# Moving the depthwise blocks behind the half-height products in a two-layer convolution kernel

## The chip, the cores and the metric

The kernel runs on one core of one Trainium2 chip, in float32 throughout. The metric is the device time of one launch in microseconds. A core has five engines that run their own instruction streams in order and wait for each other through semaphores: TensorE (PE in the profile, its weight loads PEld), VectorE (DVE), ScalarE (ACT), GpSimd (POOL) and SyncE (SP). DMAs are issued from the queues of SP, ACT and POOL.

## The reference

The input x has 8 images of 96 by 96 pixels and 192 channels. Two residual layers follow one another:

```python
x = x + L0(_gn(x), ...)   # _gn: group norm over 32 groups
x = x + L1(_gn(x), ...)
# L0: proj = x @ W_in + b_in (192 -> 384 channels); local = 3x3 depthwise conv
#     mixed = 0.25*(four exponential scans of local: left, right, down, up) + local
#     layer norm over channels; @ W_out + b_out (384 -> 192)
# L1: y = 7x7 depthwise conv + dw_bias; layer norm over the 192 channels
#     y = gelu(y @ w0 + b0) (192 -> 768); (y @ w1 + b1) * gamma (768 -> 192)
```

## The kernel before

The program is one launch, written out by hand: every queue receives its instructions in the order in which the Python code issues them (`tc.manual_schedule()`). Its stages follow one another on TensorE.

**First pass, scans and second pass.** The first pass projects to 384 channels, the next stage does the 3x3 convolution and the scans. The second pass (line 1219 on, "stage C") takes 192 steps, 3.94 us each. A step transposes three tiles to form squares, multiplies by W_out (`project_c`, L1141), and one step later `scale_c` makes the inverse deviation (VectorE, then a power on GpSimd, L1170) and `finish_c` (L1175, VectorE) scales the sums, adds the residual and frees the sums' PSUM banks; there are banks for two steps. Between `scale_c` and `finish_c` the list `steps` hands out side work, one entry a step: `bn_stats` of three groups (two in the last entry), and, once, the five single steps of `norm_c(0, ...)` (line 980: means, squares, powers, shift, spread), which make the second layer's group norm for the first half of the images.

**Depthwise blocks (stage D).** The 7x7 convolution is done in 32 blocks of 12 channels (`todo`: two halves of the images, 16 blocks each). A block n has its rows loaded (`load_raw`, three tiles t) and its band of weights (`load_band`), its rows scaled by the group norm (`scale_steps`: 24 scalings in three tiles of eight, and one copy of the band, L964), six convolutions (`conv_d`, each 24 matmuls of 64x64 tiles, L1337, and two evacuations on ScalarE, L1347), and its result stored (`store_d`). The scalings are on VectorE (L960) for most blocks and on ScalarE (L958) for block 1 and for blocks 19 and up (N1 = 19). Nineteen blocks run before the products begin, one a pass of the loop at line 1622.

**Products (stage E).** The rest of layer 1 runs in 72 units u, two to a tile n of y (loop at line 1700). For a unit, `norm_steps_e` gives seven steps of the layer norm: sums, mean, center (VectorE), square (ScalarE, L1501), squares (VectorE), powers (a VectorE sum, then a power on GpSimd, L1513, 5.4 us), scale (VectorE). They run two units ahead. `turn_in` then transposes y into yT (L1534). `first_layer` multiplies by w0 in parts: for each part first the full-height products (L1549: 128 rows by 512 columns), then the half-height products (L1559: the remaining 64 channels, two matmuls at once on the two halves of the array), then the gelus on ScalarE (L1568). `second_layer(u - 1, k)` for k = 0 to 3 multiplies by w1 (L1579); VectorE adds the residual r (L1590) and POOL issues the store. In the first 36 units `first_layer` has three parts and uses a pool of six PSUM banks, since the convolutions hold the other two; in the other 36 it has two parts and all eight banks.

**Inlaid blocks.** The last 13 depthwise blocks (19 to 31) are worked off inside stage E through the list `slots`: nine entries a block, three of scalings (called R below) and six of one convolution each (called C), and one store at the end. `slot()` is called five times a unit from u = 1 on, and each call takes the next entry, whatever it is: after the first part of `first_layer`, and after each of the four `second_layer` calls. So convolutions stand at all five places in turn.

**The passage from D to E.** In block 17's pass (n == NI + 1) the scalings of block 18 come first, then sums, mean and center of unit 0. Then the six convolutions, then the loads of tile 1 of y (`y_1`: 41 steps, eight of which at the end, the left-over channels, go through POOL). In block 18's pass unit 0's square, squares and powers, unit 1's sums, mean and center, and unit 0's scale are issued behind the third convolution. Then the rows of block 19 are loaded (POOL), and the residual r of tile 0 behind them (`load_r(0, nc.gpsimd)`); `bias_r(0)` adds a bias to it on POOL (L1430) before unit 0's loop.

Of the kernel before, what the change touches and what calls it, by code (L numbers as in the profile page):

```python
# [101 lines left out]
def conv_blocks_kernel(  # L102
# [31 lines left out]
    nc = tc.nc  # L134
# [9 lines left out]
    GS = D // GROUPS  # L144
# [437 lines left out]
    NI = len(place)  # L582
# [308 lines left out]
    NT = 3  # L891
# [53 lines left out]
    def scale_steps(n):  # L945

        hf, i = todo[n]
        steps = []

        def scale(t, k, b):  # L950
            if n not in xins:
                make_xin(n)
            c = slice(k * GS, (k + 1) * GS)
            sc, sh = (s1[:, hf, b, e, 2 * i + k : 2 * i + k + 1] for e in range(2))
            to = xins[n][:, t, b, c].rearrange("q c (a v) -> q a c v", a=NV)
            of = raws[n, t][:, b, :, c]
            if n == 1 or n >= N1:
                nc.scalar.activation(to, of, AF.Identity, bias=sh, scale=sc)  # L958
            else:
                nc.vector.tensor_scalar(to, of, sc, sh, ALU.mult, ALU.add)  # L960

        def spread():
            g, band = i % 2, bands[n]
            nc.vector.tensor_copy(  # L964
                band[(1 - g) * 64 : (2 - g) * 64], band[g * 64 : (g + 1) * 64]
            )

        for t in range(NT):
# [76 lines left out]
    with ExitStack() as ph:  # L1045
# [173 lines left out]
        with tc.manual_schedule():  # L1219
# [15 lines left out]
            for u in range(n_u + 1):  # L1235
# [23 lines left out]
                if u < n_u:  # L1259
# [7 lines left out]
                    for j in range(NJ3):  # L1267
# [1 line left out]
                        turn_c(mt, pt, j, range(0 if u else NC - 1, NC))  # L1269
                        project_c(mt, pos[j], j, ms[j])  # L1270
                        square_c(pt, pos[j], var, j)
                if steps:
                    for step in steps.pop(0):
                        step()
                if held is not None:
                    n, v = divmod(u - 1, WQ)
                    if v == 0:
                        x1c = xps[1 - n % 2].tile([128, NJ3, D, WQ], F32, tag="x1c", name="x1c")
                    finish_c(x1c, v, held[0], rs, held[2])
                    if v == WQ - 1:  # L1280
                        steps += group_steps(x1c, n)
                        stores += [
                            lambda x=x1c, n=n, j=j, q=q: store_c(x, n, j, q)
                            for j in range(NJ3)
                            for q in range(NX)
                        ]
                held = (pos, var, xr) if u < n_u else None
            for step in first_d:
                step()
# [313 lines left out]
    with tc.manual_schedule():  # L1603
        with tc.tile_pool(name="d_own", bufs=1, side="right", **by_tile) as own:
# [12 lines left out]
                NI - 5: y_0[:1],  # L1617
                NI: [y_0[1 + b * 8 + q] for q in (5, 7) for b in range(NH)]
                + y_0[1 + NH * 8 :],
                NI + 1: y_1,  # L1620
            }
            for n in range(N1):
                if n + 2 < N1:
                    for t in range(NT):
                        load_raw(n + 2, t)
                    if n:
                        load_band(n + 2)
                if n:
                    store_d(n - 1)
                if n >= 3 and norms:  # L1630
                    norms.pop(0)()
                if n == 10:
                    make_weights(bank())
                steps = scale_steps(n + 1) if n + 1 < N1 else []
                between, last = [], []
                if n == NI + 1:
                    chain = norm_steps_e(0)
                    steps += chain[:3]
                    chain = chain[3:]
                elif n == NI + 2:  # L1640
                    nxt = norm_steps_e(1)
                    between = chain[:3] + nxt[:3] + chain[3:]
                    last = nxt[3:4]
                    chain = nxt[4:]
                for step in steps:
                    step()
                for c in range(GS):
                    conv_d(n, c)
                    for step in main_y.get(n, [])[2 * c : 2 * c + 2]:
                        step(nc.gpsimd)  # L1650
                    if c == 2:
                        for step in between:
# [12 lines left out]
        tp = ctx.enter_context(tc.tile_pool(name="e_t", bufs=2, side="right", **by_tile))  # L1665

# [1 line left out]
        for n in range(N1, len(todo)):  # L1668
            more = n + 1 < len(todo)
            scales = scale_steps(n)  # L1670
            per_t = len(scales) // NT
            slots += [after + scales[:per_t], scales[per_t : 2 * per_t], scales[2 * per_t :]]
            if more:
                for t in range(NT):
                    slots[t - 3].append(lambda n=n, t=t: load_raw(n + 1, t, nc.scalar if n > N1 else None))
            slots += [[lambda n=n, c=c: conv_d(n, c, ps_y)] for c in range(GS)]
            if more:
                slots[-1].append(lambda n=n: load_band(n + 1, nc.scalar))
            after = [lambda n=n: store_d(n)]
        slots.append(after)  # L1680
# [12 lines left out]
        load_r(0, nc.gpsimd)  # L1693
        for k in range(3):
            turn_in(0, k)
        for step in chain[:2]:
# [2 lines left out]
        bias_r(0)  # L1699
        for u in range(n_u + 1):  # L1700
            n, t = divmod(u, per)
            early_half = u < n_u // 2
            parts, pool = (3, ps_h) if early_half else (2, None)
            if not early_half:
# [20 lines left out]
            if not early_half:  # L1725
# [63 lines left out]
```

## Time and profile before

The three runs of the kernel took 5416.11, 5424.39 and 5430.3 us; the median is 5424.39 us.

| | |
|---|---|
| profiled execution, own time | 5428.47 us |
| its span, first to last instruction | 5426.5 us |
| granted TensorE clock, mean | 0.986 |
| TensorE busy in the span | 97% |
| VectorE, ScalarE, GpSimd busy | 64%, 48%, 44% |
| second pass (C), first to last projection | 1801.9 to 2591.8 us |
| depthwise blocks before the products (D) | 2592.1 to about 2902 us |
| products (E), first L1549 to last L1579 | 2922.4 to 5420.4 us |
| last inlaid convolution matmul starts at | 3880.5 us |

A group of instructions in the profile is named by its line and by what it writes and reads ("L1579 PE MATMUL hp<-w1g,g"); a wait is "who waited <- whom it waited for". A matmul in float32 appears as two instructions, so a count of matmuls in the profile is twice that in the code. Ends of matmuls are modelled, so this text counts TensorE's time from start to start.

### The profile page before, as it was taken

What the parts mean: (1) busy time and instruction counts of PE and PEld (TensorE: products, weight loads), DVE (VectorE), ACT (ScalarE), POOL (GpSimd) and SP (SyncE); (2) the same over time, 40 slices, a digit from 0 to 9 for tenths busy, and PEclk for the clock granted to TensorE, in tenths of its full rate; (3) what the DMA queues carried; (4) which work ended last, traced back from release to release, by engine and by line L of the source; (5) the groups of instructions that cost most, each with busy time, mean ns of one, the idle gap of its engine ahead of it and who ended that gap; (6) DMA issues with size and microseconds to landing.
All of it is one profiled execution on the core that took longest, in us unless ns stands there. A gap on an engine that the chain in (4) does not pass through costs nothing. (4 is left out here: it accounts for less than half of the span.)

```text
span 5426.5 us, 107918 instructions
## 1 busy us (share of the span) xinstructions
PE 5247.6 (97%) x42206; PEld 3346.3 (62%) x42206; DVE 3455.9 (64%) x6722; ACT 2581.9 (48%) x5765; POOL 2405.4 (44%) x2129
## 2 busy tenths in 40 slices
PE   6999999999999999999787999999999999999999
PEld 4666643333333799999454666666666666666667
DVE  6555539999999555555556555555566666566654
ACT  2444447777777566565434444454433333323232
POOL 1111128888888555555335222233233333333332
PEclk9999989999999999999898999999999999999999
DMA  7999869999999799899998455545433233332331
GB/s 221 285 286 277 251 183 239 247 240 244 246 243 246 230 306 308 273 301 312 282 308 206 119 137 135 131 120 138 108 79 78 80 81 85 87 92 80 81 78 41
DMA packets 784651, 1015.33 MB, mean 187 GB/s; under 512 B 322359, under 2 KB 658432, under 8 KB 782096
## 3 DMA queue, kind: packets, MB, share of 16 engines
q1 hardware_dynamic: 671432, 633.30, 44.3%
q0 software_dynamic: 86896, 336.90, 18.9%
q10 hardware_dynamic: 25816, 38.25, 3.1%
q8 instruction: 334, 5.47, 0.4%
q14 instruction: 173, 1.42, 0.1%
HBM read 603.70 MB, written 420.03 MB: 189 GB/s over the span
## 5 line engine op out<-in xcount | busy, mean ns | idle before, releaser
L1579 PEld LDWEIGHTS hp<-w1g,g 128*128 128x128 f32 x6912 | 1117.9, 190 | 140.7 <-issue 78.3
L1579 PE MATMUL hp<-w1g,g 128*128 128x192 f32 x6912 | 1174.9, 329 | 0.0
L1568 ACT ACTIVATE g<-hp,b0g 128x512 f32<-128x512 f32 x864 | 519.8, 693 | 1214.8 <-PE hp L1559 1191.9
L1598 POOL DMA_DIRECT2D out_dram<-xo x288 | 211.6, 735 | 1536.8 <-DVE xo L1590 1496.9
L1590 DVE TENSOR_TENSOR xo<-hp,r 128x384 f32<-128x384 f32 x288 | 229.0, 795 | 1002.2 <-PE hp L1579 998.7
L1549 PE MATMUL hp<-yT,w0w 128*128 128x512 f32 x1728 | 779.2, 597 | 22.1 <-DVE yT L1534 21.9
L1141 PE MATMUL po<-wc,mt 128*128 128x193 f32 x3456 | 667.4, 329 | 7.4 <-DVE x1c L1175 7.3
L688 PE MATMUL pl<-pin,band 34*32 34x380 f32 (+1 forms) x13824 | 636.6, 494 | 9.6 <-DMA pin<-PL_d 4.0
L775 POOL TENSOR_TENSOR mo<-mo,z 128x768 f32<-128x768 f32 x285 | 594.6, 2086 | 4.8 <-ACT mo L713 0.6
L1141 PEld LDWEIGHTS po<-wc,mt 128*128 128x128 f32 x3456 | 556.8, 192 | 9.0 <-DVE x1c L1175 8.6
L1549 PEld LDWEIGHTS hp<-yT,w0w 128*128 128x128 f32 x1728 | 321.2, 190 | 382.3 <-issue 350.5
L721 DVE TENSOR_TENSOR_SCAN z<-decay,loc 128x768 f32<-128x768 f32 x288 | 505.9, 1757 | 61.6 <-ACT loc L697 33.0
L730 DVE TENSOR_TENSOR_SCAN z<-decay,z 128x768 f32<-128x768 f32 x288 | 498.4, 1731 | 0.1
L1337 PE MATMUL hp<-xin,band 63*64 63x372 f32 (+1 forms) x4608 | 412.7, 496 | 70.9 <-ACT yo L1347 26.9
L688 PEld LDWEIGHTS pl<-pin,band 34*32 34x32 f32 x13824 | 234.4, 108 | 393.4 <-issue 386.7
L709 PE MATMUL pa<-loc,mix 128*32 128x384 f32 x3456 | 436.5, 498 | 0.0
L712 PE MATMUL pa<-last,down 96*32 96x384 f32 x1152 | 431.4, 498 | 1.0 <-ACT mo L713 1.0
L1559 PE MATMUL hp<-yT,w0w 64*128 64x512 f32 x1728 | 419.5, 611 | 0.0
L1513 POOL TENSOR_TENSOR rs<-tot,neg_half 32x32 f32<-32x32 f32 x72 | 395.6, 5494 | 46.1 <-DVE tot L1511 45.3
L1347 ACT ACTIVATE yo<-hp,dwb 128x384 f32<-128x384 f32 x384 | 197.1, 585 | 423.4 <-PE hp L1337 290.2
L697 ACT COPY loc<-pl 128x384 f32<-128x384 f32 x576 | 248.2, 483 | 312.3 <-PE pl L688 312.3
L395 PE MATMUL pm<-xT,win 128*128 128x384 f32 x1152 | 392.2, 491 | 0.0
(159 smaller groups left out, 7276.0 us busy)
## 6 DMA issues: line engine op xcount, KB each, us to landing
P<-po POOLq DMA_DIRECT2D x96, 1152.0 KB, 9.7
pin<-P SPq DMA_DIRECT2D x190, 576.0 KB
mt<-M SPq DMA_DIRECT2D x192, 384.0 KB
xq<-in_x_dram SPq DMA_DIRECT2D x96, 576.0 KB
xr<-in_x_dram SPq DMA_DIRECT2D x192, 288.0 KB
X<-x1c SPq DMA_DIRECT2D x144, 384.0 KB
out_dram<-xo POOLq DMA_DIRECT2D x288, 192.0 KB, 2.4
r<-X SPq DMA_DIRECT2D x35, 1536.0 KB
```

The lines of the kernel that those rows point to most:

```text
L688: nc.tensor.matmul(pls[g][at * RB : (at + 1) * RB, :, lo:hi], band[rows, c, kh, :], pin[rows, c, :, NJ - 1 - j, lo + kh - 1 : hi + kh - 1] ...
L709: nc.tensor.matmul(pa[at], mix[:, i, at], loc[:, q], start=True, stop=True)
L712: nc.tensor.matmul(pa[at], down[:, to], last[:, q], start=True, stop=True)
L721: nc.vector.tensor_tensor_scan(zf, decay_f, loc.rearrange("p q n -> p (q n)"), 0.0, ALU.mult, ALU.add)
L730: nc.vector.tensor_tensor_scan(zr, decay_f, zr, 0.0, ALU.mult, ALU.add)
L775: eng.tensor_tensor(m, m, z, ALU.add)
L1141: nc.tensor.matmul(po, mt[:, m, j * 128 : (j + 1) * 128], wc[:, m], start=(m == 0), stop=(m == NC - 1),)
L1337: nc.tensor.matmul(pys[g][k * 64 : (k + 1) * 64, :, lo:hi], band[rows, k * GS + c, d * ZS : d * ZS + 64], xin[rows, :, :, k * GS + c, lo + ...
L1549: nc.tensor.matmul(hps[m, q], w0w[:, 0, m * 128 : (m + 1) * 128], yT[:, 2 * q], start=True, stop=False,)
L1559: nc.tensor.matmul(hps[m, q], w0w[p, 1, m * 128 : (m + 1) * 128], yT[p, 1], start=False, stop=True,)
L1568: nc.scalar.activation(g[:, m, q], hps[m, q], AF.Gelu, bias=b0g[:, m : m + 1], scale=1.0)
L1579: nc.tensor.matmul(po[:, q], g[:, m, q, k * 128 : (k + 1) * 128], w1g[:, m], start=(m == 0), stop=(m == NE - 1),)
```

## The change

There are four edits.

1. **Kinds of slots and new places.** Entries of `slots` are marked "rows" or "conv", and a call of `slot` takes the next entry only if its kind is among those that it names. Convolutions may now stand behind each of the three parts of `first_layer`, that is, right behind half-height products, and behind `second_layer(u - 1, 2)`. Rows may stand behind `second_layer` 0, 1, 2 and 3. The loads that `slot` also issued are issued by `some()` at the five old places.
2. **When the three parts end.** `first_layer` has three parts, and six banks, as long as `slots` is not empty at the start of a unit, instead of up to unit 35.
3. **The passage from D to E.** The last eight scalings of block 18 go from VectorE to ScalarE and are issued two behind each of the first four convolutions of block 17. Unit 0's square, squares and powers, unit 1's sums, mean and center, and unit 0's scale are issued before the convolutions of block 18, not behind the third. The eight left-over loads of y's tile 1 on POOL go from the end of block 17's pass to the end of block 18's, behind the powers. The rows of block 19 are loaded behind r of tile 0, not ahead of it.
4. **Second pass.** An entry of `steps` that holds a single step (the five of `norm_c(0)`) is issued behind `finish_c`, the others ahead of it as before.

```diff
-            if n == 1 or n >= N1:
+            if n == 1 or n >= N1 or (n == N1 - 1 and t == NT - 1):
                 nc.scalar.activation(to, of, AF.Identity, bias=sh, scale=sc)
...
-                if steps:
-                    for step in steps.pop(0):
+                now = steps.pop(0) if steps else []
+                if len(now) > 1:
+                    for step in now:
                         step()
                 if held is not None:
...
+                if len(now) == 1:
+                    now[0]()
                 held = (pos, var, xr) if u < n_u else None
...
-                NI + 1: y_1,
+                NI + 1: y_1[:-8],
...
                 if n == NI + 1:
                     chain = norm_steps_e(0)
-                    steps += chain[:3]
+                    per_t = len(steps) // NT
+                    between = steps[-1 - per_t : -1]
+                    steps = steps[: -1 - per_t] + steps[-1:] + chain[:3]
                     chain = chain[3:]
                 elif n == NI + 2:
                     nxt = norm_steps_e(1)
-                    between = chain[:3] + nxt[:3] + chain[3:]
-                    last = nxt[3:4]
+                    steps = chain[:3] + nxt[:3] + chain[3:]
+                    last = y_1[-8:] + nxt[3:4]
                     chain = nxt[4:]
...
-                    if c == 2:
-                        for step in between:
-                            step()
+                    for step in between[2 * c : 2 * c + 2]:
+                        step()
...
-            for t in range(NT - 1):
-                load_raw(N1, t)
...
-        load_raw(N1, NT - 1)
...
-        def slot():
+        def slot(*kinds):
 
-            if slots and u >= 1:
-                for step in slots.pop(0):
+            if slots and u >= 1 and slots[0][0] in kinds:
+                for step in slots.pop(0)[1]:
                     step()
+
+        def some():
+
             for step in loads[:14]:
                 step()
             del loads[:14]
 
         load_r(0, nc.gpsimd)
+        for t in range(NT):
+            load_raw(N1, t)
...
-            early_half = u < n_u // 2
-            parts, pool = (3, ps_h) if early_half else (2, None)
+            inlaid = bool(slots)
+            parts, pool = (3, ps_h) if inlaid else (2, None)
...
             first_layer(u, 0, parts, pool)
             chain.pop(0)()
-            slot()
+            slot("conv")
+            some()
...
             second_layer(u - 1, 0, pool)
             norm.pop(0)()
             chain.pop(0)()
-            slot()
-            if early_half:
+            slot("rows")
+            some()
+            if inlaid:
                 first_layer(u, 1, parts, pool)
+                slot("conv")
             turn_in(u + 1, 0)
             second_layer(u - 1, 1, pool)
             chain.pop(0)()
-            slot()
+            slot("rows")
+            some()
...
             second_layer(u - 1, 2, pool)
             turn_in(u + 1, 1)
             chain.pop(0)()
-            slot()
+            slot("rows", "conv")
+            some()
...
-            if early_half:
+            if inlaid:
                 first_layer(u, 2, parts, pool)
+                slot("conv")
             chain.pop(0)()
             second_layer(u - 1, 3, pool)
             chain.pop(0)()
-            slot()
+            slot("rows")
+            some()
```

More of the change, by code (lines that the diff above doesn't have):

```diff
@@ L1671, in conv_blocks_kernel @@
             per_t = len(scales) // NT
-            slots += [after + scales[:per_t], scales[per_t : 2 * per_t], scales[2 * per_t :]]
+            slots += [
+                ("rows", after + scales[:per_t]),
+                ("rows", scales[per_t : 2 * per_t]),
+                ("rows", scales[2 * per_t :]),
+            ]
             if more:
                 for t in range(NT):
-                    slots[t - 3].append(lambda n=n, t=t: load_raw(n + 1, t, nc.scalar if n > N1 else None))
-            slots += [[lambda n=n, c=c: conv_d(n, c, ps_y)] for c in range(GS)]
+                    slots[t - 3][1].append(lambda n=n, t=t: load_raw(n + 1, t, nc.scalar if n > N1 else None))
+            slots += [("conv", [lambda n=n, c=c: conv_d(n, c, ps_y)]) for c in range(GS)]
             if more:
-                slots[-1].append(lambda n=n: load_band(n + 1, nc.scalar))
+                slots[-1][1].append(lambda n=n: load_band(n + 1, nc.scalar))
             after = [lambda n=n: store_d(n)]
-        slots.append(after)
+        slots.append(("rows", after))
         loads = []
-        def slot():
-            if slots and u >= 1:
-                for step in slots.pop(0):
+        def slot(*kinds):
+            if slots and u >= 1 and slots[0][0] in kinds:
+                for step in slots.pop(0)[1]:
                     step()
+        def some():
             for step in loads[:14]:
@@ L1701, in conv_blocks_kernel @@
             n, t = divmod(u, per)
-            early_half = u < n_u // 2
-            parts, pool = (3, ps_h) if early_half else (2, None)
-            if not early_half:
+            inlaid = bool(slots)
+            parts, pool = (3, ps_h) if inlaid else (2, None)
+            if u >= n_u // 2 - 4:
                 assert not slots
@@ L1721, in conv_blocks_kernel @@
             chain.pop(0)()
-            slot()
+            slot("rows")
+            some()
             if t == 1 and n + 1 < n_y:
                 bias_r(n + 1)
-            if not early_half:
+            if not inlaid:
                 first_layer(u, 1, parts, pool)
```

## The prediction

> **What bounds the kernel now.** I read the page first (engines, costliest groups), then sums by stretch, then TensorE's timeline inside stage E, then the waits at the two places where TensorE stands still.
>
> ```profile
> PE 5247.6 (97%) x42206; PEld 3346.3 (62%) x42206; DVE 3455.9 (64%) x6722; ACT 2581.9 (48%) x5765; POOL 2405.4 (44%) x2129
> ```
>
> ```profile
> 2592.00:2922.00 330.00, 247.75 (x2773) 152.28 (x2772) 193.28 (x535) 131.50 (x259) 116.90 (x158) 0.88 0.96 282
> 2941.00:2987.00 46.00, 39.44 (x192) 24.09 (x190) 27.17 (x52) 26.78 (x46) 32.71 (x30) 0.93 0.65 159
> 2987.00:3904.00 917.00, 913.24 (x5145) 568.41 (x5138) 491.40 (x974) 439.14 (x764) 262.89 (x137) 1.00 0.52 128
> ```
>
> The columns of the second view are the stretch, its length, busy time of PE, PEld, DVE, ACT, POOL, then clock, DMA share, GB/s. TensorE is the bound. In D it idles 82 us of 330, with DMA at 0.96; in the inlaid part it idles under 4 us of 917. What can be won there lies in the order of matmuls, not in waits. Unit 8, and then unit 9, on TensorE's timeline (start, length):
>
> ```profile
> 3232.50 1.99 PE L1559 MATMUL hp<-yT,w0w 64*128 64x512 f32 x8
> 3234.41 2.13 PE L1337 MATMUL hp<-xin,band 63*64 63x384 f32 x24
> 3236.47 4.17 PE L1579 MATMUL hp<-w1g,g 128*128 128x192 f32 x24
> 3240.47 3.60 PE L1549 MATMUL hp<-yT,w0w 128*128 128x512 f32 x8
> 3244.00 1.99 PE L1559 MATMUL hp<-yT,w0w 64*128 64x512 f32 x8
> ```
>
> ```profile
> 3273.02 4.17 PE L1579 MATMUL hp<-w1g,g 128*128 128x192 f32 x24
> 3277.12 2.12 PE L1337 MATMUL hp<-xin,band 63*64 63x384 f32 x24
> 3279.18 3.70 PE L1549 MATMUL hp<-yT,w0w 128*128 128x512 f32 x8
> 3282.81 1.99 PE L1559 MATMUL hp<-yT,w0w 64*128 64x512 f32 x8
> ```
>
> Start to start: a convolution takes 2.06 us in both places. Behind half-height products (3232.50 to 3234.41) they keep their 1.91 us, as where second products follow (1.92). Between full-height matmuls, the 24 second products ahead take 4.10 instead of 4.00 (3236.47 to 3240.47) and the first products behind 3.63 instead of 3.53. So a convolution costs 2.06 us behind half-height products and 2.26 elsewhere. Unit starts on the same timeline give the rest: a unit without convolutions takes 32.24 us with three parts (units 25 to 35) and 31.85 with two (36 on).
>
> The passage from D to E, and the second pass around 2250 us, as waits (us, times, longest):
>
> ```profile
> PE hp L1549 <- DVE yT L1534: 21.9, 2, 20.4
> POOL yb L1404 <- DMA yb<-Y: 20.1, 2, 17.7
> POOL r L1430 <- DMA r<-X: 14.9, 1, 14.9
> DVE s L1507 <- ACT sq L1501: 5.9, 1, 5.9
> ```
>
> ```profile
> PE po L1141 <- DVE x1c L1175: 7.3, 4, 3.3
> ```
>
> TensorE waits 20.4 us for unit 0's yT and 7.3 us for `finish_c`. POOL's timeline tells why yT is late: the power stands behind loads that wait.
>
> ```profile
> 2909.05 2.28 POOL L1404 DMA_DIRECT2D yb<-Y  x4 [17.67 <-DMA yb<-Y]
> 2911.40 6.21 POOL L1513 TENSOR_TENSOR rs<-tot,neg_half 32x32 f32<-32x32 f32 x1
> ```
>
> **What the Trainium skill says.** TensorEngine Tiling (Array Packing), Key Properties: a change of tiling mode drains TensorE, a change of tile does not. The trace agrees for full to split (0.10 us each way) and shows nothing for 64x128 to 64x64. TensorE: Matmul & The Clock Gate, Part 1: after about 3.4 us of idleness the array runs at half clock until it has been busy as long. The trace agrees: the stretch 2240 to 2272 has clock 0.89. DMA: Bandwidth & Descriptors, Queues, rings and completion order: an engine takes turns between queues, and each queue has its own ring. So r, issued behind six row loads on POOL's queue, should land late: 26.4 us after issue, where the row loads' median is 13.0.
>
> **The change part by part**, against the span of 5426.5 us.
>
> *Places.* Taking 9 entries a block through the new calls, a block fills two units: odd units hold C (first part), R, R, R, C (third part); even units C, C, C (behind second products 2), C. The queue empties in unit 27 (before: 24). Behind half-height products stand 65 convolutions of 78 (before 15; count of the five places). 15 x 2.06 + 63 x 2.26 = 173.3 us becomes 65 x 2.06 + 13 x 2.26 = 163.3: **-10.0**.
>
> *Three parts.* Units 28 to 35 get two: 8 x 0.39 = **-3.1**.
>
> *Stalls in the inlaid part.* Units 2 to 24 last 916.5 us (2987.3 to 3903.8); 23 x 32.24 + 15 x 2.06 + 61 x 2.26 = 910.3. The rest, 6.2, is in units 5, 10, 14, 19, 23, where a block's first C comes one second product (4 us) behind its last R: in unit 5 L1337 waits 1.09 us for ACT's scalings and then runs slower. The new order has a whole part, 5.45 us, between them. That is a new wait, once a block; behind it on PE queue second product 3 and the next unit. Units 8 and 17 already have R, R, R at these places: in unit 8 the scalings end at 3258.82 (3255.21 + 3.60), the band copy at 3257.34, the third part at 3259.27. Margin 0.45 us, so **-6.2**; without it, up to 13 x 1.5 = +20. PSUM: the tightest pair is C behind second product 2 and C behind the third part; in unit 9 ACT has evacuated at 3298.2 and the third part ends at 3302.6.
>
> *Passage.* Center of ya ends at 2895.25 (2894.02 + 1.23); its start hangs on loads that are not moved. Now ACT does six evacuations first, waiting for block 16's store until 2896.48, and the squares run 2899.27 to 2902.22. New: block 17's evacuations and 8 scalings (8 x 0.45 = 3.6 us, mostly in pauses of 0.84 between pairs) end near 2891.8, so squares take 2895.3 to 2898.3, the reduce 1.75, the sum 1.6: 2901.7. POOL has no loads ahead: power until 2907.1 to 2907.9. VectorE does unit 1's sums, mean, center meanwhile (7.9, from 2905.61 to 2913.48 now): 2909.6. Scale 3.6, first transpose 1.04: TensorE starts at 2914.3, not 2922.37: **-8.1**. Block 18's evacuations queue behind the squares and cost its fifth convolution 1 to 2 us; it ends near 2903, hidden by the wait for yT. VectorE's relief (8 x 0.30) is hidden by the y loads that sums wait for.
>
> POOL then issues 8 loads (4.5 us), r (1.2), six row loads (3.7): done near 2917, before unit 1's power (2919.5, 5.1 us after TensorE's start as now). r takes rows' old place: its buffer was block 18's rows, read by 2890. At the 130 GB/s that the 3.9 MB of rows and r had (2917.6 to 2947.9), r lands near 2925, rows by 2943; ScalarE needs the first at about 2940. So `bias_r` ends near 2930 instead of 2953.3, and unit 2's power no longer stands behind it. Unit 1 takes 46.74 us, of which 32.24 + 2.27 + 2.16 are explained: 10.1 lost, among it 1.55 for yT (which stays: the chain from unit 1's power is unchanged) and 4.86 for the band copy that comes late behind unit 2's scale. I keep 2.5: **-7.6**. Bounds: 0 (row loads, now last, hold ScalarE) and -10.
>
> *Second pass.* Steps 109 to 113 start at 2241.40 and end at 2274.01: 32.6 us for 5 x 3.944, so 12.9 lost, 1.6 of it matmuls of the norm. Squares (2.8 us on VectorE) no longer stand ahead of `finish_c`: the wait of 3.32 goes. The power of 5.44 us on POOL starts near 2250.9, behind `finish_c`, and the next inverse deviation waits behind it until 2256.4: TensorE then waits about 3.8 us where it waited 2.26. With 0.4 before, 2 of slow clock and 1.6 of matmuls, 7.8 remain: **-5.1**. Bounds -9 and +1.
>
> Sum: -10.0 - 3.1 - 6.2 - 8.1 - 7.6 - 5.1 = -40.1. Span 5386.4; own time (2.0 above its span) 5388.4. The median shown is 4.1 below that execution; I keep the distance: **5384 us**.
>
> **Rivals.**
> *The passage's gain is lost again.* The left-over loads, r and rows share DMA with blocks 17 and 18's stores (share 0.89 at 2910 to 2930); late ones hold `sums` of unit 2 or ScalarE in unit 1. For: the 0.89. Against: VectorE's chain, not DMA, sets unit 1's yT. Then the 15.7 of the passage go: -24.4, 5400.
> *The first C of a block waits.* If ACT or VectorE runs 1 to 2 us later than in unit 8, 13 blocks lose 0.5 to 1.5 each: 7 to 20 us, 5391 to 5404. Against: the margin measured above.
> *Slower.* Convolutions close behind each other wait for ScalarE, which does four gelus (2.42 us) before each pair of evacuations. It decides from (40.1 + 16.3) / 65 = 0.87 us a convolution: above 5441. Against: the tightest slack is 4.4 us, and ACT is busy 439 of 917.
> *It does not do what it says*: were the queue not empty by unit 32, an assertion would stop the build; the count says 27.
>
> **How the numbers follow.** What a measurement can tell is about 0.3%, 16.3 us: below 5408.1 is faster, above 5440.7 slower. The forecast has 0.62, with its own range 5376 to 5394 (the bounds of -5.1 and -7.6, mostly). Lost passage 0.17, waiting first C 0.10, slower 0.05. The remaining 0.06 is for what I don't see, mostly smaller gains. Faster 0.62 + 0.17 + 0.10 less 0.03 for several losses together = 0.86; same 0.08; slower 0.06. The range 5374 to 5408 takes in the first three cases.
>
> **What would show it.** Right: even units of 41.0 us (32.24 + 3 x 2.06 + 2.26, and neighbours' 0.1), odd 36.4; units 28 to 35 at 31.85; last convolution in unit 27; TensorE's first L1549 about 13 us earlier than 2922.4 in the span (8.1 and the second pass's 5.1); L1430 waiting under 5 us for r; unit 1 near 37. Wrong: L1337 waiting for ACT xin or band once a block; L1513 still late at 2907 (less 5); a wait of PE po for x1c above 6 us in the second pass; or half-height to convolution costing 0.1 where unit 8 shows none.

## The result and the profile after

| | before | after |
|---|---|---|
| median of the first comparison, 6 runs each | 5420.25 us | 5394.46 us |
| its ratio, 95% interval | | 0.9962 (0.9946 to 0.9979) |
| median of a later comparison, 24 and 19 runs | 5415.18 us | 5401.21 us |
| its ratio, 95% interval | | 0.9975 (0.9966 to 0.9985) |
| profiled execution, own time | 5428.47 us | 5391.33 us |
| its span | 5426.5 us | 5389.5 us |

The changed kernel is faster, by 8 to 18 us (about a quarter of a per cent) in the comparison with more runs. Both medians lie in the predicted range (5374 to 5408). The 37 us between the two profiled spans are more than the change is worth, as the next table shows, so the total alone would have been read wrongly. TensorE's starts divide the span into stretches (us; "109 to 113" are the second pass's steps with the norm; "block 17 to E" runs from block 17's first convolution to the first product):

| stretch | before | after | difference | predicted |
|---|---|---|---|---|
| scans (code unchanged) | 1046.0 | 1038.6 | -7.4 | 0 |
| second pass without steps 109 to 113 (unchanged) | 757.5 | 753.1 | -4.4 | 0 |
| depthwise stage up to block 17 (unchanged) | 285.0 | 276.5 | -8.5 | 0 |
| steps 109 to 113 | 32.6 | 27.0 | -5.6 | -5.1 |
| block 17 to E | 45.3 | 38.0 | -7.3 | -8.1 |
| units 0 and 1 | 64.9 | 63.6 | -1.3 | -10.0 |
| units 2 to 27 | 1013.2 | 1013.7 | +0.5 | -13.7 |
| units 28 to 35 | 258.0 | 254.8 | -3.2 | -3.1 |
| units 36 to 71 (unchanged) | 1168.0 | 1168.1 | +0.1 | 0 |

The predicted column splits the -10.0 of the places as the blocks lie: 2.4 in units 0 and 1, where one convolution stands instead of two, and 7.5 in units 2 to 27. Stretches with unchanged code give 20 of the 37 us. They vary from one execution to the next: over all profiles of this study the scans take 1036 to 1058 us. Units 2 to 27 hardly do: 1013.2, 1013.2 and 1013.0 in three profiles of the old order. So what follows compares stretches, not totals.

The lines named here from L1337 on are numbered three higher in the changed kernel: L1337 is L1340 there, L1549 L1552, L1559 L1562, L1579 L1582, L1430 L1433, L1501 L1504, L1513 L1516, L1534 L1537 and L1590 L1593. The 24 matmuls of a convolution are counted as in the profile; the code has 12.

The page of the changed kernel, engines in the span:

```profile
PE 5228.0 (97%) x42206; PEld 3347.5 (62%) x42206; DVE 3469.5 (64%) x6714; ACT 2579.8 (48%) x5773; POOL 2412.2 (45%) x2129
```

And three of its stretches: depthwise stage to the first product, units 2 to 27, units 28 to 35 (stretch, length, busy time of PE, PEld, DVE, ACT, POOL, clock, DMA share, GB/s):

```profile
2575.00:2889.00 314.00, 248.25 (x2772) 149.46 (x2771) 190.66 (x527) 134.38 (x267) 110.15 (x151) 0.89 0.97 291
2953.00:3966.00 1013.00, 1003.54 (x5589) 638.92 (x5589) 564.58 (x1104) 470.06 (x806) 313.53 (x159) 1.00 0.49 125
3967.00:4221.00 254.00, 254.00 (x1150) 176.54 (x1149) 158.01 (x336) 79.80 (x112) 93.23 (x48) 1.00 0.32 83
```

The middle line is the surprise. TensorE idles 9.5 us in units 2 to 27, although each convolution there costs less. The waits of that stretch (us, times, longest) name who holds it:

```profile
PE hp L1340 <- ACT xin L958: 7.6, 9, 1.1
PE hp L1340 <- DVE band L964: 1.3, 2, 0.6
```

Most blocks have one such wait, at the convolution behind the third part of an odd unit. Even units take 40.66 to 40.67 us, and 32.24 + 3 x 2.06 + 2.26 is 40.68: the cheaper place is as cheap as predicted. Odd units should take 36.36 (32.24 + 2 x 2.06) and take 37.05 to 37.98. Twelve of them lose 14.4 us together, more than the 13.7 that was to be won here. Unit 9 from its third part on, all engines in order of start:

```profile
3250.60 2.77 ACTq L926 DMA_DIRECT2D raw<-X  x2
...
3251.49 1.22 DVE L1482 TENSOR_TENSOR yb<-yb,m 128x1024 f32<-128x1024 f32 x1
3251.54 6.47 POOL L1433 TENSOR_TENSOR r<-r,b1g 128x3072 f32<-128x3072 f32 x1
...
3253.42 2.07 ACT L1504 ACTIVATE sq<-ya 128x1024 f32<-128x1024 f32 x1 [2.85 <-DVE yb L1482]
...
3255.28 1.11 ACT L1504 ACTIVATE sq<-yb 128x512 f32<-128x512 f32 x1
3255.42 3.91 DVE L964 COPY band<-band 64x2496 f32<-64x2496 f32 x1
...
3256.20 3.57 ACT L958 ACTIVATE xin<-raw,s 128x192 f32<-128x192 f32 x8
...
3256.85 1.99 PE L1562 MATMUL hp<-yT,w0w 64*128 64x512 f32 x8
...
3259.47 2.46 PE L1340 MATMUL hp<-xin,band 63*64 63x384 f32 x24 [0.63 <-DVE band L964]
```

The half-height products end at 3258.84. Two things that the convolution needs end later: the band copy at 3259.33, which takes 3.91 us where it takes 1.46 in units without POOL's L1433 beside it, and the last scalings on ScalarE at 3259.77. Both suspects were tested apart.

The other place that fell short is the end of unit 0, when TensorE waits for unit 1's yT (timeline of the changed kernel, all engines):

```profile
2906.63 5.59 DVE L1472 COPY m<-tot 32x64 f32<-32x64 f32 x2
...
2906.75 5.42 POOL L1433 TENSOR_TENSOR r<-r,b1g 128x3072 f32<-128x3072 f32 x1 [5.06 <-DMA r<-X]
...
2912.79 1.03 DVE L1537 STREAM_TRANSPOSE yT<-ya 128x512 f32<-128x512 f32 x1
...
2913.97 2.04 PE L1552 MATMUL hp<-yT,w0w 128*128 128x512 f32 x2 [5.29 <-DVE yT L1537]
```

Two copies of unit 2's mean that take 0.38 us together elsewhere take 5.59, and end when the bias of r on POOL ends. The transposes for unit 1 stand behind them on VectorE's queue. r, now loaded ahead of the rows, let that bias start 17.4 us after TensorE's first product, not 25.5.

### The profile page after: what moved, and what is told of

It is laid out like the page before. It is cut to its first block, busy times and chain, and to the rows that moved or that the text cites. A ratio compares the mean times of both kernels' runs of the same rounds, so it can differ in the third digit from the quotient of the medians.

```text
span 5389.5 us, 107959 instructions
## 1 busy us (share of the span) xinstructions
PE 5228.0 (97%) x42206; PEld 3347.5 (62%) x42206; DVE 3469.5 (64%) x6714; ACT 2579.8 (48%) x5773; POOL 2412.2 (45%) x2129
## 4 chain that ended last, share of the span: by engine, by line
PE 84%; DMA 5%; issue 3%; DVE 2%; SPq 2%; ACT 1%; POOL 1%; ACTq 0%; POOLq 0%; DVEq 0%
PE hp L1582 19%; PE hp L1552 12%; PE pl L688 11%; PE po L1141 10%; PE hp L1562 7%; PE pm L395 6%; PE pa L709 5%; PE hp L1340 4%; PE pt L1135 3%; PE pm L408 3%; DMA Y<-yo 3%; PE pa L712 2%; PE pt L381 2%; DMA mt<-M 1%; ACT xin L958 1%
## 5 line engine op out<-in xcount | busy, mean ns | idle before, releaser
L1582 PEld LDWEIGHTS hp<-w1g,g 128*128 128x128 f32 x6912 | 1118.5, 190 | 116.4 <-issue 61.1
L1582 PE MATMUL hp<-w1g,g 128*128 128x192 f32 x6912 | 1168.4, 329 | 0.0
L1593 DVE TENSOR_TENSOR xo<-hp,r 128x384 f32<-128x384 f32 x288 | 228.8, 794 | 973.4 <-PE hp L1582 969.1
L1552 PE MATMUL hp<-yT,w0w 128*128 128x512 f32 x1728 | 777.4, 597 | 17.1 <-DVE yT L1537 17.1
L688 PE MATMUL pl<-pin,band 34*32 34x380 f32 (+1 forms) x13824 | 632.2, 491 | 10.7 <-issue 6.6
L1552 PEld LDWEIGHTS hp<-yT,w0w 128*128 128x128 f32 x1728 | 324.3, 191 | 362.6 <-issue 355.2
L1340 PE MATMUL hp<-xin,band 63*64 63x372 f32 (+1 forms) x4608 | 412.6, 494 | 64.9 <-DMA band<-Z_d 23.0
L1516 POOL TENSOR_TENSOR rs<-tot,neg_half 32x32 f32<-32x32 f32 x72 | 392.2, 5447 | 65.3 <-DVE tot L1514 55.3
L1562 PE MATMUL hp<-yT,w0w 64*128 64x512 f32 x1728 | 417.4, 610 | 0.0
L1340 PEld LDWEIGHTS hp<-xin,band 63*64 63x64 f32 x4608 | 213.2, 137 | 263.9 <-issue 131.9
```

What stands on the lines that cost most here:

```text
L688: nc.tensor.matmul(pls[g][at * RB : (at + 1) * RB, :, lo:hi], band[rows, c, kh, :], pin[rows, c, :, NJ - 1 - j, lo + kh - 1 : hi + kh - 1] ...
L1340: nc.tensor.matmul(pys[g][k * 64 : (k + 1) * 64, :, lo:hi], band[rows, k * GS + c, d * ZS : d * ZS + 64], xin[rows, :, :, k * GS + c, lo + ...
L1552: nc.tensor.matmul(hps[m, q], w0w[:, 0, m * 128 : (m + 1) * 128], yT[:, 2 * q], start=True, stop=False,)
L1562: nc.tensor.matmul(hps[m, q], w0w[p, 1, m * 128 : (m + 1) * 128], yT[p, 1], start=False, stop=True,)
L1582: nc.tensor.matmul(po[:, q], g[:, m, q, k * 128 : (k + 1) * 128], w1g[:, m], start=(m == 0), stop=(m == NE - 1),)
```

## The experiments

All edits are to the changed kernel unless said otherwise. "Bias" is `bias_r`, POOL's L1433. Where no median is given, a kernel was run once, so that its stretches are compared and not its total.

### Two suspects for the waiting convolution

The bias left out:

```diff
-        bias_r(0)
...
-            if t == 1 and n + 1 < n_y:
-                bias_r(n + 1)
```

> The changed kernel without the second layer's output bias: bias_r, the POOL addition of 5.4 us over r, is left out everywhere (for units 0 and later). The sum that is left out is the bias b1 times gamma. Theory P[...]: VectorE's band copy L964 and unit 0's copy of the mean last 3.9 and 5.4 us because POOL's bias_r runs at the same time. Then every band copy takes 1.46 us, unit 0's copy 0.4, TensorE's wait of 5.3 us for yT in unit 0 goes, and odd units fall from 37.1-38.0 to 36.4 us. Theory A (ScalarE late): the first convolution waits for ScalarE's last scalings, which are held by row loads issued between them. Then the copies may become short, but odd units keep at least 0.7 us of their loss, 37.1 or more.

The row loads on ScalarE's queue moved from the scalings to the convolutions:

```diff
             if more:
                 for t in range(NT):
-                    slots[t - 3][1].append(lambda n=n, t=t: load_raw(...))
...
             slots += [("conv", [lambda n=n, c=c: conv_d(n, c, ps_y)]) for c in range(GS)]
             if more:
+                for t in range(NT):
+                    slots[t - 5][1].append(lambda n=n, t=t: load_raw(...))
```

> The changed kernel, but the loads of the next block's rows are issued from ScalarE's queue behind the second, third and fourth convolution of a block, not between its scalings. Theory P: band copies stay at 3.9 us in odd units and L1340 still waits for DVE band; odd units lose 0.6 to 0.7 us instead of 1.2 on average (the start of the copy and its length don't move). Theory A: the wait goes, odd units take 36.4 us.

Both, with the bias not left out but issued in even units:

```diff
-            if t == 1 and n + 1 < n_y:
-                bias_r(n + 1)
+            if t == 0 and 0 < n < n_y:
+                bias_r(n)
```

> As the run before, and bias_r for a tile is issued in the tile's own even unit (at the same place), not in the odd unit before it, which holds the band copy. Nothing is left out. Theories P and A together: band copies 1.46 us, odd units 36.4 us, units 2 to 27 about 14 us shorter than in the changed kernel (1013.7). If odd units stay above 37, something else is late. Unit 0's wait for yT (5.3 us) stays, since the first bias_r is not moved.

| | changed | no bias | loads moved | both |
|---|---|---|---|---|
| band copy L964, us | 3.9 | 1.46 | 3.9 | 1.46 |
| units 2 to 27, us | 1013.7 | 1012.1 | 1007.0 | 999.2 |

Without the bias the copy is short, and the stretch gains only 1.6: the long copy was not all that held the convolution. The timeline of that kernel in unit 9:

```profile
3271.80 2.77 ACTq L926 DMA_DIRECT2D raw<-X  x2
3274.62 2.04 ACT L1504 ACTIVATE sq<-ya 128x1024 f32<-128x1024 f32 x1 [2.85 <-DVE yb L1482]
3276.45 1.11 ACT L1504 ACTIVATE sq<-yb 128x512 f32<-128x512 f32 x1
3276.57 1.46 DVE L964 COPY band<-band 64x2496 f32<-64x2496 f32 x1
...
3277.36 3.57 ACT L958 ACTIVATE xin<-raw,s 128x192 f32<-128x192 f32 x8
...
3278.06 1.99 PE L1562 MATMUL hp<-yT,w0w 64*128 64x512 f32 x8
...
3280.54 2.55 PE L1340 MATMUL hp<-xin,band 63*64 63x384 f32 x24 [0.50 <-ACT xin L958]
```

Now ScalarE alone holds it. Issuing two loads takes 2.77 us; the square behind them starts late, and the last scalings behind the square. The convolution starts late and, as the scalings reach it piecemeal, takes 2.55. With the loads moved instead, the band copy holds it (timeline of that kernel, unit 9):

```profile
3255.15 6.46 POOL L1433 TENSOR_TENSOR r<-r,b1g 128x3072 f32<-128x3072 f32 x1
...
3259.03 3.90 DVE L964 COPY band<-band 64x2496 f32<-64x2496 f32 x1
...
3260.47 1.99 PE L1562 MATMUL hp<-yT,w0w 64*128 64x512 f32 x8
...
3263.08 2.12 PE L1340 MATMUL hp<-xin,band 63*64 63x384 f32 x24 [0.62 <-DVE band L964]
```

Each cause alone keeps a large part of the 14.4 us: 12.9 without the bias, 7.8 with the loads moved. With both gone, TensorE waits for neither, and the stretch takes 999.2: my sum of 999.5 for it was right but for these two.

The same by another way: start the slots one unit later, so that scalings stand in even units, where the bias isn't:

```diff
-            if slots and u >= 1 and slots[0][0] in kinds:
+            if slots and u >= 2 and slots[0][0] in kinds:
```

> The changed kernel with the first slot taken in unit 2, not 1: a block's scalings and band copy now stand in even units, which have no bias_r and the loads of y only at their end; four convolutions stand in odd units. Theories P and A: the units with scalings take 36.4 us, those with four convolutions 40.7, band copies 1.46; the list is empty in unit 28 (one more unit of three parts, +0.4). Units 1 to 35 are 13 us shorter than in the changed kernel. A rival in which the wait comes from the place itself, a whole part behind the last scaling being too short, keeps 37.1 to 38.0 in these units.

Units 2 to 27 took 999.6 us. The list empties one unit later, and units 28 to 35 take 257.2 for 254.8. Units 0 and 1 kept their wait for yT (5.7 us), as nothing had been done about it. Units 1 to 35 together are 10.7 us shorter than in the changed kernel, not the 13 expected: one convolution moved from unit 1 to unit 28, but unit 1 got no shorter by it (39.95 us for 39.02). The place of the entries, with no load taken from the scalings, is enough: the load ahead of the square takes 1.9 to 2.75 us to issue in the changed kernel, and 0.63 in nine of eleven blocks there. Why the issue of a load on ScalarE's queue is so uneven stays open.

### What took unit 1's gain

The bias of tile 0 moved to the end of unit 0, behind unit 2's power:

```diff
-        bias_r(0)
         for u in range(n_u + 1):
...
             second_layer(u - 1, 3, pool)
             chain.pop(0)()
+            if u == 0:
+                bias_r(0)
             slot("rows")
```

> The changed kernel, but the first bias_r is issued on POOL at the end of unit 0, behind the power of unit 2, not ahead of the loop. Theory P: VectorE's copy of unit 2's mean takes 0.4 us instead of 5.6, yT of unit 1 is ready 5.2 us earlier, and units 0 and 1 together take about 5 us less than 63.6. Rival (the chain from unit 1's power alone sets yT): no change in TensorE's wait of 5.3 us.

The wait for yT fell to 1.9 us. But the first convolution of block 19, in unit 1, waited 3.4 us for ScalarE's scalings, so units 0 and 1 took 59.2 us: near the 58.6 expected here, but not the 55 of the prediction's sum. Without any bias (the first experiment) the wait is 1.0 and the two units take 55.6, close to that sum. The rows ahead of r again, as before the change:

```diff
-        load_r(0, nc.gpsimd)
         for t in range(NT):
             load_raw(N1, t)
+        load_r(0, nc.gpsimd)
```

> The changed kernel with the six row loads of block 19 ahead of r of tile 0 again, nothing else. My theory (unit 1's gain was lost because r, loaded first, lands 13 to 20 us after TensorE's first product and starts its bias on top of VectorE's copies for unit 2): r lands and the bias starts at 20 us or later, TensorE's wait for yT at the end of unit 0 falls from 5.3 to 6.8 us to 2 or less, and units 0 and 1 together take 56 to 60 us instead of 64. Rival (the order of the loads doesn't matter; the wait comes from unit 0 beginning earlier): 62 or more. Units 2 to 27 stay at 1012 to 1014 by both.

The wait for yT fell to 2.0 us, as my theory said, and yet the two units took 63.0: its number failed, and the rival's (62 or more) came true, though not for the rival's reason. The timeline of this kernel in units 0 and 1, cut to what matters:

```profile
2924.58 5.44 POOL L1433 TENSOR_TENSOR r<-r,b1g 128x3072 f32<-128x3072 f32 x1 [16.66 <-DMA r<-X]
...
2929.97 5.43 POOL L1516 TENSOR_TENSOR rs<-tot,neg_half 32x32 f32<-32x32 f32 x1
...
2935.43 0.38 DVE L1472 COPY m<-rs 32x64 f32<-32x64 f32 x2 [4.59 <-POOL rs L1516]
...
2947.62 3.57 ACT L958 ACTIVATE xin<-raw,s 128x192 f32<-128x192 f32 x8
...
2950.80 2.78 PE L1340 MATMUL hp<-xin,band 63*64 63x384 f32 x14 [4.65 <-ACT xin L958]
```

r landed 28.2 us after the first product. Its bias then ran ahead of unit 2's power; unit 2's scale on VectorE, the next unit's square on ScalarE and the scalings behind it came late. So the bias of tile 0 can hurt in two ways. Too early, it holds VectorE ahead of unit 1's transposes (starts at 13.2 to 18.7 us: waits for yT of 5.3 to 7.1, five profiles; what it holds is a copy of unit 2's mean, or of unit 1's inverse deviation, or the subtraction of unit 2's mean, L1482, as each comes first). Too late, it holds unit 2's power (25.5 before the change, with a wait of 4.86 for the first convolution, and 28.3 here). In between (20.4 to 22.2, three profiles), neither costs over 2.3 us. With the order of the changed kernel r was seen to land anywhere from 13.1 to 20.3; why it varies so is not shown, so unit 1's loss is in part a matter of chance.

### Parts of the change alone

Each of these is the kernel before with one part of the change. Edit 4 alone:

```diff
+                if len(now) == 1:
+                    now[0]()
                 held = (pos, var, xr) if u < n_u else None
```

> The kernel before with the edit of the second pass alone. Steps 109 to 113 of the second pass take 27.0 us as in the changed kernel, not 32.6; the rest of the pass and stages D and E are those of the kernel before up to what DMA does from run to run. A rival in which the shorter second pass of the changed kernel (10 us) is all the edit's would give 780 us from the first L1141 to the first L1337, not 785.

Edits 1 and 2 alone, with the rows of block 19 ahead of r as before:

```diff
-        def slot():
+        def slot(*kinds):
...
-            early_half = u < n_u // 2
-            parts, pool = (3, ps_h) if early_half else (2, None)
+            inlaid = bool(slots)
+            parts, pool = (3, ps_h) if inlaid else (2, None)
```

> The kernel before with the new places of the inlaid blocks and the early end of three parts alone. Even units 40.7, odd units 37.1 to 38.0 as in the changed kernel, band copies in odd units 3.9 us; units 28 to 35 at 31.85. Units 2 to 35 then last 3 us less than before (1271.2), not the 19 that the switches and stalls promised. Unit 0 as before (18.2), unit 1 about 44: it keeps the late r and has one convolution less.

Edit 3 alone:

```diff
-                    between = chain[:3] + nxt[:3] + chain[3:]
-                    last = nxt[3:4]
+                    steps = chain[:3] + nxt[:3] + chain[3:]
+                    last = y_1[-8:] + nxt[3:4]
...
         load_r(0, nc.gpsimd)
+        for t in range(NT):
+            load_raw(N1, t)
```

> The kernel before with the passage from D to E alone. From block 17's first convolution to the first L1549 about 38 us as in the changed kernel, not 45; unit 0 about 24 us, with TensorE waiting 5 us for yT while POOL's bias_r holds VectorE's copy; unit 1 about 39 to 41 with two convolutions. Units 0 and 1 together stay near 64, so that the edit gains about 7 us and not the 15.7 that I counted.

| stretch, us | before | edit 4 | edits 1, 2 | edit 3 |
|---|---|---|---|---|
| steps 109 to 113 | 32.6 | 27.0 | 31.0 | 32.6 |
| block 17 to E | 45.3 | 47.3 | 40.8 | 38.4 |
| units 0 and 1 | 64.9 | 59.4 | 56.5 | 66.4 |
| units 2 to 27 | 1013.2 | 1013.2 | 1012.1 | 1013.0 |
| units 28 to 35 | 258.0 | 258.0 | 254.8 | 258.0 |

Units 2 to 27 and 28 to 35, which hardly vary, and steps 109 to 113, whose old form takes 31.0 to 32.6, answer to their own edits. The other two rows vary too much without an edit to be read from one profile each. Over all profiles, steps 109 to 113 take 32.1 us in the old form (mean of 3) and 26.8 in the new (10): -5.3. Block 17 to E takes 44.5 (3) and 38.6 (11): -5.9, in which the old form alone varies by 6.5 (40.8 to 47.3), so this gain is known only roughly. Units 0 and 1 differ where their code does not, 59.4 against 64.9 before, because r lands at 21.2 instead of 25.4: the first convolution of block 19 waits 2.22 us instead of 4.86, and the matmuls behind that wait don't run slow. What the prediction took as a fixed loss of before was a matter of when a load arrived. Two expectations missed by it: unit 1 with edits 1 and 2 took 37.8, not 44, as r landed at 22.1; and with edit 3 the two units took 66.4, with a wait for yT of 7.0, so that they took back 1.5 of what the passage gained.

### The two causes mended together, and the last wait of the second pass

Slots from unit 2 on, and tile 0's bias at the end of unit 0: the fourth and the fifth edit together.

> The changed kernel with two edits: the slots start in unit 2 instead of 1, so that the rows entries stand in even units and never beside POOL's bias of r, and the bias of r of tile 0 stands at the end of unit 0, behind unit 2's power. My theory (the first convolution of a block waits because rows entries meet that bias; unit 1's gain was lost because tile 0's bias ran on top of VectorE's copies): units 2 to 27 take about 999.6 us (1013.7 in the changed kernel), units 28 to 35 257 (one more unit with three parts), units 0 and 1 together 54 to 57 (63.6), in all some 19 to 21 us below the changed kernel's span by these stretches, so 5370 to 5377 as a median. Rival (the two waits are one loss that turns up elsewhere once it is pushed aside, as a late band copy did when the bias alone was moved): units 0 and 1 stay at 59 or more, or units 2 to 27 at 1007 or more, and the median stays above 5380.

To that, the group norm's power on POOL, 32 columns, is cut into four entries of 8:

```diff
-            nc.gpsimd.tensor_tensor(rb[:, 0], ve, neg_half[:, :GROUPS], ALU.pow)
+            t["ve"] = ve
+
+        def power(k):
+            g = slice(k * GROUPS // 4, (k + 1) * GROUPS // 4)
+            nc.gpsimd.tensor_tensor(rb[:, 0, g], t["ve"][:, g], neg_half[:, g], ALU.pow)
...
-        return [means, squares, powers, shift, spread]
+        return [means, squares, powers] + [lambda k=k: power(k) for k in range(4)] + [shift, spread]
```

> The run before with one more edit: the power of the second pass's group norm, 32 columns on POOL in one instruction of 5.44 us, is cut into four of 8 columns, one a step (used in the depthwise stage too, where it has time). My theory (the 3.46 us that TensorE still waits in steps 109 to 113 are the next inverse deviation standing behind this power): those steps, now up to 116, lose that wait, so 109 to 113 take 22 to 24 us instead of 26.9, and the total falls by some 3 us, which single executions can't show. Rival (the wait is the norm's own matmuls and the slow clock behind them): the five steps stay at 26 or more, or the steps up to 116 lose as much as was won.

And the changed kernel once more, without an edit:

> The changed kernel once more, unedited, timed beside the two others and the kernel before. Theory: 0.996 of the kernel before, within 0.002; in the profile units 2 to 27 take 1013 to 1014 us, units 28 to 35 254.8, units 0 and 1 together 62 to 65, and the steps 109 to 113 about 27. Rival (the profiled execution of the changed kernel was a chance): one of these stretches differs by more than 2 us.

| | after, again | two mends | and the power cut |
|---|---|---|---|
| median, us | 5401.21 (19 runs) | 5381.91 (6) | 5373.66 (5) |
| ratio to before, interval | 0.9975 (0.9966 to 0.9985) | 0.9943 (0.9926 to 0.9961) | 0.9913 (0.9897 to 0.9928) |
| steps 109 to 113, us | 27.1 | 26.8 | 20.8 |
| units 0 and 1 | 64.7 | 56.3 | 53.3 |
| units 2 to 27 | 1012.3 | 999.8 | 999.8 |
| units 28 to 35 | 254.8 | 257.2 | 257.2 |

The changed kernel came out as expected (a ratio of 0.996, within 0.002): the stretches that the change touches lie within 1.4 us of those of its first profile. Both mends hold together: in units 2 to 27 TensorE has no wait left that the profile shows. The median of the mended kernel, 5381.9, is above the 5370 to 5377 that I expected and above the rival's mark of 5380; but it is 19.3 below the changed kernel timed beside it, where I had 19 to 21, and the stretches that I had named came out as expected (56.3 and 999.8). What was off is the level from which I had counted. Of the wait left in the second pass, the POOL timeline of the changed kernel shows the cause:

```profile
2244.61 5.44 POOL L1020 TENSOR_TENSOR gn_rb<-gn_ve,neg_half 128x32 f32<-128x32 f32 x1
2250.01 0.86 POOL L1170 TENSOR_TENSOR rs<-ve,neg_half 128x3 f32<-128x3 f32 x1
```

The inverse deviation of the next step stands behind the norm's power, and TensorE waits 3.46 us for banks that `finish_c` frees only with it. TensorE's wait in the changed kernel, then in the kernel with the power cut, where these lines are numbered four higher (us, times, longest):

```profile
PE po L1141 <- DVE x1c L1175: 3.9, 2, 3.5
```

```profile
PE po L1145 <- DVE x1c L1179: 0.5, 1, 0.5
```

POOL with the power cut:

```profile
2255.40 1.65 POOL L1024 TENSOR_TENSOR gn_rb<-gn_ve,neg_half 128x8 f32<-128x8 f32 x1
2257.78 0.85 POOL L1174 TENSOR_TENSOR rs<-ve,neg_half 128x3 f32<-128x3 f32 x1 [0.73 <-DVE ve L1172]
```

The five steps fall from 26.8 to 20.8, below the 22 to 24 expected. Step 116, where the last matmuls of the norm now stand, takes 0.85 more than the usual 3.94; so the cut is worth about 5 us. All five runs of this kernel are below all six of the mended one without the cut; it is 47 us (39 to 56) below before. Of the 8 us between these two medians, 3 lie in units 0 and 1, where the code is the same.

## Why the prediction was right, and where it was wrong

The direction and the range held. Of the six terms three held, a fourth (the passage) as far as the spread lets one tell, and two failed.

- **Three parts, -3.1**: -3.2. Exact, as it came from whole units.
- **Second pass, -5.1**: -5.3 over the profiles. The new wait was foreseen as 3.8 us, behind POOL's power, and measured 3.46.
- **Passage, -8.1**: -7.3 in the pair, -5.9 as a mean, where the old form alone varies by 6.5. The first product's wait fell from 20.4 to 10.7 us; the chain is as described.
- **Places, -10.0**: the price was right. Even units are 40.67 us for 40.68 summed (the 41.0 given as a sign of being right is more than its own terms add up to), and half-height to convolution costs nothing more. With the stalls away (999.2 to 999.8) the whole term is there.
- **Stalls in the inlaid part, -6.2**: this step failed. It rested on "Margin 0.45 us", read in unit 8. Unit 8 is even; in the new order the scalings always fall into odd units, where two things differ: the bias on POOL runs beside the band copy, and ScalarE's load issues are longer. Neither margin stood. The loss was 14.4 us where I had 0, 1.2 for each of 12 blocks. The rival that named this had 0.5 to 1.5 and 7 to 20 us, but I gave it 0.10 and argued against it with the same unit; its mark, L1337 (now L1340) waiting for xin or band about once a block, is the first that the prediction names for being wrong. Unit 17 of before, which I named and didn't read, has scalings in an odd unit and shows the long copy (VectorE's timeline of the kernel before):

```profile
3615.36 3.89 DVE L964 COPY band<-band 64x2496 f32<-64x2496 f32 x1
```

It ends at 3619.25, behind the third part's 3618.78, and did no harm there, as that unit's next convolution came one second product later (3622.80). Reading it would have shown one cause of the two: its loads ahead of the square took 1.25 us together, not 2.77.

- **Unit 1, -7.6**: this step failed too. It came to its bound of 0 in effect (units 0 and 1 together -1.3 and, in the second profile, -0.3, of which the one convolution less is -2.4), though not by the row loads that the bound named. I had r land 10.7 us after the first product at 2914.3 and `bias_r` end "near 2930", some 15 us after it, and asked only whom it no longer holds on POOL. I did not ask what VectorE does while it runs. It starts at 17.4, as r landed only then, 15.3 us after its issue, and the wait for yT "which stays" at 1.55 went to 5.29. In the second profile r was issued 2.2 us before the first product, and its bias, at 13.2, met VectorE's copies all the same (6.8). Nor was the loss of before a fixed one: it depended on when r landed.

The two failed terms lost 22 to 23 us of the 40.1, and no total showed it. By the stretches that the change touches it is worth 17 us in the pair, and 13.5 (8 to 18) by the comparison with more runs. So the forecast's 40 was more than twice too large, and that the median lies in the range does not confirm the sum: the range was made wide enough for the rivals. The sum's own range, 5376 to 5394, just misses the first median (5394.46), where unchanged stretches of the profiled run were 20 us shorter by chance, and misses the later one (5401.21) by more. Where the medians came out belongs to the rival of the waiting convolution (5391 to 5404), whose mechanism the experiments show. The rival of the lost passage (5400, given 0.17) came true by half: unit 1's gain went, but to a bias that came early, not to loads that came late.

## What to carry to other kernels

A margin read in one repetition holds for those that have the same neighbours; when work moves to other repetitions, read the margin there, on every engine that supplies it. When an engine off the path gets its data earlier, look at what else runs in its new place; here it was POOL's addition beside VectorE's copies. Judge a change of a few tenths of a per cent by the stretches that it touches, with the untouched ones as a measure of chance.

## What the hardware showed that I had not expected

**POOL's bias and VectorE's copies exclude each other.** The Trainium skill says so (SBUF — State Buffer, section "SBUF: two separate sides"): VectorE and GpSimd share a pair of ports under an exclusive lock; a VectorE operation in a two-port mode, or one with two inputs in SBUF against a GpSimd operation that reads SBUF, and GpSimd's operation wait for each other for a whole instruction. The traces agree for the bias. In unit 9, the bias ends at 3258.01 and the copy, issued at 3255.42, ends 1.32 us later, about its own 1.46. All 12 band copies that met the bias took 3.9 us, and so did the one of before; no other took over 1.6. The profile shows none of this as a wait: the operation that comes second only gets longer. The other way round, the bias takes 6.47 us instead of 5.42 when it is issued while L1482 runs (until 3252.71), which subtracts the mean from y and reads two tensors in SBUF. In the kernel with the loads moved and the bias in even units, L1482 came 0.3 us behind the bias of tile 0 and took 6.18 instead of 1.22 (VectorE's timeline at the end of unit 0):

```profile
2920.73 6.18 DVE L1482 TENSOR_TENSOR ya<-ya,m 128x1024 f32<-128x1024 f32 x1
```

**Not every operation takes part.** Transposes (L1537, 46 that met the bias) kept their 1.06 us, and L1593, whose one input is in PSUM, its 0.8 (32). POOL's power (L1516) held up none of the ten copies that met it in the changed kernel; they kept 0.17 to 0.18 us, though copies of the same lines were held by the bias. The page's rule names no such exception, so here the measurement differs from it. Why the power differs from the bias is not shown.

**A power on POOL is priced by its columns**: 0.86 us for 3, 1.65 for 8, 5.44 for 32 (on 128 rows, and about the same on 32), or 0.4 + 0.16 a column by these three, so cutting one in four costs 1.2 us of POOL and shortens the longest hold from 5.4 to 1.65.
